# A convolution network on one core: who evicts which step of the tap matrices, where pending norms, gate weights and the sigmoid table stand

## The chip, the core and the metric

The kernel runs on one core of a Trainium2 chip. The metric is the time of one execution on the device in microseconds; the median of the runs counts. A profiled execution gives a trace besides.

## The reference, cut to what matters

An image batch of 4 images, 256 channels, 56 x 56 in fp32 goes through four layers. Each normalizes in groups of channels and adds its result to its input.

```python
x = x + involution(_gn(x), reduce_w, reduce_b, span_w, span_b)     # layer 0: 7x7, 16 groups
x = x + conv3x3_block(_gn(x), w1, bn1, w2, bn2)                    # layer 1: two 3x3 convolutions
x = x + involution_bn(_gn(x), w1, bn1, w2, b2, bn2)                # layer 2: 7x7, 16 groups, norms, relu
x = x + gates(_gn(x), W, b)                                        # layer 3
```

An involution computes, for each group of 16 channels and each pixel, its own 7 x 7 kernel (two 1 x 1 convolutions of the input, `kern = span_w @ h + span_b`), and sums `kern * patches` over the 49 taps. Layer 3 has a gate by channel, `sigmoid(cf @ W.T + b)`, where `cf` is the real mean of a Fourier transform over the image and so the image's first pixel, and a gate by pixel, the real Fourier transform of the mean over channels; the output is `x * cf + x * sf`.

## The kernel before, in words

**Units and stages.** `involution_layer` runs twice, with layer 0 and with layer 2; between them `conv_layer` does layer 1. An involution works through 8 units: 4 images b, and of each two blocks cb of 128 channels. Below, unit 0 to 7 of a layer is unit `2 * b + cb`. A unit has two stages.

*Tap phase* (`tap_matrices`, L560). 32 steps n = 0..31. In each, TensorE makes six matmuls (L571) from `z_sb` and `hp` into a PSUM tile of two banks (`two_banks`); then the tile is evicted into `kt` with the bias `zb_sb` added. Every third step, those with `n % 3 == 0` (L579), ScalarE evicts in six activations (L582); in the others VectorE does in one addition (L589). After step n, the hooks of n are called: small pieces of other work, put there by hand with `place(hooks, g, at)`. A generator g makes its next piece at each place of the list.

*Apply stage* (`apply`, L601). For each of 7 column strips tx, 112 matmuls (L613) of `xw` and `kt` go into two PSUM tiles; ScalarE (L626 or L628) and VectorE (L633, L640) or GpSimd (L638) bring the result into the image block. After each strip `next_windows` transposes a later strip (L398), ScalarE copies it to `xw` (L399), and DMAs of SP and GpSimd fill the shifted windows (L405, L407); `next_strip` normalizes the next strip, on GpSimd in layer 0 (L381) and on ScalarE in layer 2 (L379). Column statistics (`column_sums`, L1067) go to VectorE.

**PSUM.** One pool `banks` has 4 slots of two banks. The steps, the small matmuls of the hooks (`one_bank` takes a whole slot) and the apply stage share it.

**Order.** `in_order` fixes the order of each engine as the program is written, so that an instruction that waits holds up all behind it on its engine.

**The hooks that matter.** `norm_steps` (L200 to L223) makes the group norm of a block in six pieces: aggregate on VectorE (L204), matmul (L207), four VectorE operations (L210 to L215), matmul (L218), the inverse root on VectorE and GpSimd (L138, L139), shift (L222). Its places for the block just finished are steps 2, 6, 7, 11, 12, 13 (L989). In layer 0, units 1, 3 and 5 also make the norm of the next image's first block. In units 1 and 2 of layer 2 the norms of the last image of layer 1 that are still pending have the places 19, 20, 22, 23, 25, 26 (L990 to L992).

In layer 2 `channel_mean` (L668) makes, at steps 13 and 17, the mean over channels of the block that has just been finished: matmuls (L696), two ScalarE activations (L704), and two stores by SP (L707) with a load back (L708) into `m2_of`. `gate_factors` (L711) makes an image's gates when both of its blocks are finished, that is in units 2, 4 and 6: at step 17 it loads the 256 x 256 weights `w3` in two DMAs of 128 KB on SP (L716), at 24 it multiplies them with the first pixels (L723) and ScalarE applies the sigmoid (L730), at 27, 28, 30 and 31 it makes the gate by pixel (L739 to L763). The weights lie in a dead part of the image block (`dead`, L660), which must first be stored (L1082) and summed over channels (L696). The next image's load (L275) takes that block later. `gate_chunk` (L768) applies the gates to stored blocks on GpSimd in pieces of 8 rows during the units that follow; its gate map `sfb` (L773, L774) has two buffers.

The last image's gate factors have their first place at step 20 of unit 7 and their second after the last apply stage.

At its start, layer 0 has a ScalarE copy (L310) ahead of all else on that engine.

Of the kernel before, what the change touches and what calls it, by code (L numbers as in the profile page):

```python
# [10 lines left out]
F32 = mybir.dt.float32  # L11
AF = mybir.ActivationFunctionType
# [4 lines left out]
P = 128  # L17
B, C, H, W = 4, 256, 56, 56
NB = C // P
# [52 lines left out]
def net_kernel(  # L72
# [207 lines left out]
    def involution_layer(layer, xin, xout, red, span, sb, xs_of, ahead=None, pending=None):  # L280

        with ExitStack() as es:
# [23 lines left out]
            if layer == 0:  # L306
                load(0, 0, (2, 2, 2, 1))
                load(0, 1, (2, 2, 2, 1))

                nc.scalar.copy(norm_sb[:, 3, B - 1, 1, :], mhalf)  # L310

            red_sb = wpool.tile([P, NB, 2, R], F32, name="red_sb")

# [246 lines left out]
            def tap_matrices(b, cb, hooks):  # L560

                hp = h_of[b]
                kt = big.tile([Q, GB, TP // PB, NT, PB], F32, name="kt")
                for n in range(GB // 2 * TP // PB):
                    gp, pb = divmod(n, TP // PB)
                    ps = two_banks()
                    for k in range(PB):
                        py, px = divmod(pb * PB + k, TX)
                        z0 = ZF - py * QX - px
                        for i in range(2):  # L570
                            nc.tensor.matmul(  # L571
                                ps[:Q, i, k * NT : (k + 1) * NT],
                                z_sb[i * R : (i + 1) * R, cb * GB // 2 + gp, z0 : z0 + Q],
                                hp[i * R : (i + 1) * R, py, px].rearrange("p a t -> p (a t)"),
                                start=True,
                                stop=True,
                            )
                    g0, p0 = 2 * gp, pb * PB
                    if n % 3 == 0:  # L579
                        for i in range(2):  # L580
                            for k in range(PB):
                                nc.scalar.activation(  # L582
                                    kt[:, g0 + i, pb, :, k],
                                    ps[:Q, i, k * NT : (k + 1) * NT],
                                    AF.Identity,
                                    bias=zb_sb[:, cb * GB + g0 + i, p0 + k : p0 + k + 1],
                                )
                    else:
                        nc.vector.tensor_tensor(  # L589
                            kt[:, g0 : g0 + 2, pb],  # L590
                            ps[:Q, :, : PB * NT].rearrange("q i (k t) -> q i t k", k=PB),
                            zb_sb[:, cb * GB + g0 : cb * GB + g0 + 2, p0 : p0 + PB]
                            .unsqueeze(2)
                            .to_broadcast([Q, 2, NT, PB]),
                            ALU.add,
                        )
                    for h in hooks.get(n, ()):
                        h()
                return kt
# [68 lines left out]
            def channel_mean(b, cb):  # L668
# [39 lines left out]
                nc.sync.dma_start(m2_of[cb], m_dram[b][cb].rearrange("j (r w) -> (j r) w", w=W))  # L708
                yield

            def gate_factors(b):  # L711


                w3_sb = [dead(b, 1, 4 * CR * W + ci * C, C) for ci in range(NB)]
                for ci in range(NB):
                    nc.sync.dma_start(w3_sb[ci], w3[ci * P : (ci + 1) * P])  # L716
                cf = small.tile([P, NB], F32, name="cf")
                cf_of[b] = cf
                yield
                for co in range(NB):  # L720
                    ps = one_bank()
                    for ci in range(NB):
                        nc.tensor.matmul(  # L723
                            ps[:, 0:1],
                            w3_sb[ci][:, co * P : (co + 1) * P],
                            first_of[b][:, ci : ci + 1],
                            start=(ci == 0),
                            stop=(ci == NB - 1),
                        )
                    nc.scalar.activation(  # L730
                        cf[:, co : co + 1], ps[:, 0:1], AF.Sigmoid, bias=cp[:, co, L3_B : L3_B + 1]
                    )
                yield

                ps = one_bank()
                for i in range(2):
                    at = slice(i * R, i * R + W)
                    for cb in range(NB):
                        nc.tensor.matmul(  # L739
                            ps[at, :H],  # L740
                            m2_of[cb],
                            sin_sb if i else cs2_sb[:H],
                            start=(cb == 0),
                            stop=(cb == NB - 1),
                        )
                yield
                for i in range(2):
                    at = slice(i * R, i * R + W)
                    nc.vector.tensor_copy(half[at], ps[at, :H])
                yield  # L750

                ps = one_bank()
                nc.tensor.matmul(ps[:H, :W], half, cs2_sb, start=True, stop=True)
                scale = small.tile([P, NB], F32, name="gscale")
                bias = small.tile([P, NB], F32, name="gbias")
                nc.vector.tensor_mul(scale, cf, norms[3][b][0])
                nc.vector.tensor_scalar_add(scale, scale, 1.0)
                nc.vector.tensor_mul(bias, cf, norms[3][b][1])
                gate_of[b] = scale, bias
                yield  # L760
                sf = small.tile([H, W], F32, name="sf", bufs=1)
                nc.vector.tensor_copy(sf, ps[:H, :W])
                nc.sync.dma_start(sf_dram[b].rearrange("j (r w) -> (j r) w", w=W), sf)  # L763
                yield
# [3 lines left out]
            def gate_chunk(b, j, cb):  # L768

                rstd, shift = norms[3][b]  # L770
                at = slice(j * CR * W, (j + 1) * CR * W)
                if cb == 0:
                    sf_of[b] = work.tile([P, CR * W], F32, name="sfb", bufs=2)  # L773
                    nc.gpsimd.dma_start(sf_of[b], sf_dram[b][j : j + 1].to_broadcast([P, CR * W]))  # L774
                sf = sf_of[b]
                xs = gx_tile()
                nc.gpsimd.dma_start(xs, xout[b][cb][:, at])
                yield
                xn = work.tile([P, CR * W], F32, name="gn", bufs=1)
                nc.gpsimd.tensor_scalar(  # L780
                    xn, xs, rstd[:, cb : cb + 1], shift[:, cb : cb + 1], ALU.mult, ALU.add
                )

                scale, bias = (t[:, cb : cb + 1] for t in gate_of[b])
                nc.gpsimd.tensor_scalar(xs, xs, scale, bias, ALU.mult, ALU.add)
                nc.gpsimd.tensor_tensor(xn, xn, sf, ALU.mult)
                nc.gpsimd.tensor_tensor(xs, xs, xn, ALU.add)
                nc.gpsimd.dma_start(ov[b, cb][:, at], xs)
                yield
# [140 lines left out]
            def place(hooks, g, at):  # L930

                for n in at:
                    hooks.setdefault(n, []).append(step(g))
# [50 lines left out]
            for u, (b, cb) in enumerate(units):  # L984
                hooks = hooks0 if u == 0 else {}
                if prev is not None:
                    pb, pc, st, last_sums = prev
                    hooks.setdefault(1, []).append(last_column(last_sums))
                    place(hooks, norm_of(layer + 1, pb, pc, st), (2, 6, 7, 11, 12, 13))  # L989
                    if layer == 2 and u < 3:  # L990
                        g = norm_of(2, B - 1, u - 1, pending[1][u - 1])
                        place(hooks, g, (19, 20, 22, 23, 25, 26))  # L992
                    if layer == 2:
                        place(hooks, channel_mean(pb, pc), (13, 17))
                        if pc == 1:
                            place(hooks, gate_factors(pb), (17, 24, 27, 28, 30, 31))
                        elif pb == B - 1:
                            factors = gate_factors(pb)
                            place(hooks, factors, (20,))
                            hooks.setdefault(21, []).append(lambda pb=pb: last_dft(pb))  # L1000
                            hooks.setdefault(22, []).append(last_ones)
                            place(hooks, first_half(pb), (28, 29))
                    if layer == 2 and cb == 1 and b > 0:
                        for n in (16, 22, 28):
                            hooks.setdefault(n, []).extend((next_gate, next_load))
# [705 lines left out]
```

## Time and profile before

| | us |
|---|---|
| median of 3 runs | 1826.7 (1824.32 to 1828.33) |
| profiled execution, device time | 1834.67 |
| its span | 1832.9 |
| layer 0, first tap matmul | 39.19 |
| layer 2, first tap matmul | 1266.1 |
| tap phase of units 1, 2 of layer 0 | 25.12, 23.69 |
| tap phases of units 1 to 7 of layer 2 | 30.71, 35.20, 27.53, 30.64, 27.65, 33.39, 28.42 |

A tap phase is counted from the start of its first matmul record (L571) to the start of its last one. The mean granted clock of TensorE is 0.976 of full speed.

A line of a timeline has the start (us from the span's start), how long the group took, engine, line of the kernel, operation, output and inputs with their sizes, how many instructions, and in brackets the idle time of the engine before it and what ended it. PE is TensorE's matmul, PEld its load of weights, DVE VectorE, ACT ScalarE, POOL GpSimd, SP SyncE. A line of the costliest groups has the busy time and the mean duration in ns, then the idle time of the engine just before the group. A line of a table by stretches has the stretch, its length, each engine's busy time with its number of instructions (PE, PEld, DVE, ACT, POOL), the granted clock, the share of the DMA engines and GB/s. Durations come from the one profiled execution.

### The profile page before, as it was taken

What the parts mean: (1) busy time and instruction counts of PE and PEld (TensorE: products, weight loads), DVE (VectorE), ACT (ScalarE), POOL (GpSimd) and SP (SyncE); (2) the same over time, 40 slices, a digit from 0 to 9 for tenths busy, and PEclk for the clock granted to TensorE, in tenths of its full rate; (3) what the DMA queues carried; (4) which work ended last, traced back from release to release, by engine and by line L of the source; (5) the groups of instructions that cost most, each with busy time, mean ns of one, the idle gap of its engine ahead of it and who ended that gap; (6) DMA issues with size and microseconds to landing.
All of it is one profiled execution on the core that took longest, in us unless ns stands there. A gap on an engine that the chain in (4) does not pass through costs nothing.

```text
span 1832.9 us, 55841 instructions
## 1 busy us (share of the span) xinstructions
PE 1726.3 (94%) x24034; PEld 1518.9 (83%) x24034; DVE 1379.0 (75%) x2729; ACT 845.9 (46%) x1981; POOL 429.6 (23%) x626
## 2 busy tenths in 40 slices
PE   7999999999889999999999999997999899999888
PEld 6898889888878988998899889885877777887776
DVE  3787777776589988898888988874777677677674
ACT  3566556565533222223123212114667567576554
POOL 2333432245210000000000000000000563672681
PEclk9999999999989999999999999998999999999996
DMA  2545534454651101111111210222533665764743
GB/s 84 156 154 161 175 111 149 142 159 141 185 175 47 58 35 58 68 58 51 50 60 61 73 36 33 79 90 66 159 124 128 202 200 168 216 217 131 201 140 105
DMA packets 66003, 215.75 MB, mean 118 GB/s; under 512 B 13237, under 2 KB 20926, under 8 KB 62046
## 3 DMA queue, kind: packets, MB, share of 16 engines
q1 hardware_dynamic: 48718, 145.24, 25.3%
q0 software_dynamic: 14688, 64.78, 11.0%
q8 instruction: 189, 3.10, 0.7%
q10 hardware_dynamic: 2352, 2.18, 0.4%
q14 instruction: 56, 0.46, 0.1%
HBM read 76.30 MB, written 49.15 MB: 68 GB/s over the span
## 4 chain that ended last, share of the span: by engine, by line
PE 77%; DVE 9%; ACT 6%; DMA 4%; issue 2%; SPq 1%; POOL 0%; ACTq 0%; DVEq 0%; POOLq 0%
PE mm L1482 19%; PE ps L571 17%; PE ps L613 16%; PE mm L1400 10%; PE mm L1371 5%; PE ps L398 4%; ACT kt L582 3%; DMA xw<-xw 3%; PE ps L450 2%; DVE kt L589 2%; DVE un L633 1%; ACT xw L399 1%; ACT hp L469 1%; DVE res L1475 1%; PE ps L696 1%
## 5 line engine op out<-in xcount | busy, mean ns | idle before, releaser
L613 PE MATMUL ps<-kt,xw 126*32 126x48 f32 (+1 forms) x12544 | 382.5, 236 | 46.3 <-issue 18.8
L613 PEld LDWEIGHTS ps<-kt,xw 126*32 126x32 f32 (+1 forms) x12544 | 343.5, 122 | 91.7 <-issue 51.5
L571 PE MATMUL ps<-hp,z_sb 64*126 64x133 f32 x6144 | 392.3, 281 | 14.8 <-ACT kt L582 6.8
L571 PEld LDWEIGHTS ps<-hp,z_sb 64*126 64x126 f32 x6144 | 369.7, 187 | 33.2 <-ACT kt L582 12.2
L1482 PE MATMUL mm<-v,u_sb 128*128 128x280 f32 (+1 forms) x1728 | 385.0, 384 | 3.5 <-DVE v L1307 3.5
L589 DVE TENSOR_TENSOR kt<-ps,zb_sb 126x798 f32<-126x798 f32 x336 | 319.8, 982 | 90.4 <-PE ps L571 89.9
L1482 PEld LDWEIGHTS mm<-v,u_sb 128*128 128x128 f32 x1728 | 327.5, 190 | 57.9 <-DVE v L1307 3.8
L582 ACT ACTIVATE kt<-ps,zb_sb 126x133 f32<-126x133 f32 x1056 | 307.5, 442 | 94.6 <-PE ps L571 94.0
L1400 PE MATMUL mm<-v,u_sb 128*128 128x252 f32 (+1 forms) x936 | 212.4, 388 | 3.5 <-DVE v L1291 3.5
L1400 PEld LDWEIGHTS mm<-v,u_sb 128*128 128x128 f32 x936 | 178.0, 191 | 34.2 <-issue 3.5
L633 DVE SCALAR_TENSOR_TENSOR un<-ps,s,un 128x240 f32<-128x240 f32 x224 | 102.5, 458 | 97.0 <-ACT un L628 92.8
L1519 POOL DMA_DIRECT2D x<-xs x24 | 13.1, 547 | 683.2 <-DVE xs L1518 427.4
L633 DVE SCALAR_TENSOR_TENSOR un<-ps,par_sb,un 128x240 f32<-128x240 f32 x224 | 98.2, 457 | 90.9 <-ACT un L626 86.7
L1467 ACT ACTIVATE res<-xs,shift,norm_sb 128x1120 f32<-128x1120 f32 (+1 forms) x24 | 30.2, 1259 | 235.6 <-DVE xs L1518 107.3
L399 ACT COPY xw<-ps 126x896 f32<-126x896 f32 x112 | 101.7, 908 | 48.6 <-PE ps L398 40.8
L638 POOL TENSOR_TENSOR xs<-un,xs 128x240 f32<-128x240 f32 x112 | 72.3, 666 | 199.4 <-DVE un L633 199.4
L398 PE MATMUL ps<-ident_sb,strip_sb 128*126 128x128 f32 x784 | 112.1, 284 | 0.2 <-DVE un L633 0.2
L626 ACT ACTIVATE un<-ps,par_sb 128x240 f32<-128x240 f32 x112 | 50.3, 449 | 120.6 <-PE ps L613 115.5
L628 ACT ACTIVATE un<-ps,bn_t,s 128x240 f32<-128x240 f32 x112 | 60.2, 539 | 93.1 <-PE ps L613 89.9
L139 POOL TENSOR_TENSOR norm_sb<-norm_sb,mhalf 128x1 f32<-128x1 f32 x32 | 19.8, 620 | 344.1 <-DVE norm_sb L138 344.1
L1371 PE MATMUL mm<-xs,u_sb 128*128 128x126 f32 (+1 forms) x792 | 98.5, 277 | 1.3 <-DVE xs L1334 0.9
L1371 PEld LDWEIGHTS mm<-xs,u_sb 128*128 128x128 f32 x792 | 94.4, 191 | 2.4 <-issue 1.0
(254 smaller groups left out, 2000.6 us busy)
## 6 DMA issues: line engine op xcount, KB each, us to landing
xw<-xw SPq DMA_DIRECT2D x168, 252.0 KB
xw<-xw SPq DMA_DIRECT2D x224, 126.0 KB
xw<-xw POOLq DMA_DIRECT2D x56, 252.0 KB, 4.6
xs<-x SPq DMA_DIRECT2D x24, 560.0 KB
x<-xs POOLq DMA_DIRECT2D x8, 1568.0 KB, 8.0
xs<-x SPq DMA_DIRECT2D x8, 1568.0 KB
xs<-in_x_dram SPq DMA_DIRECT2D x6, 1568.0 KB
x<-xs SPq DMA_DIRECT2D x6, 1568.0 KB
```

The costliest lines, as they stand in the source:

```text
L398: nc.tensor.transpose(ps[:Q, k * P : (k + 1) * P], flat[:, k * Q : (k + 1) * Q], ident_sb)
L399: nc.scalar.copy(xw[:, :NSB, :], ps[:Q, : NSB * P].rearrange("q (n c) -> q n c", n=NSB))
L571: nc.tensor.matmul(ps[:Q, i, k * NT : (k + 1) * NT], z_sb[i * R : (i + 1) * R, cb * GB // 2 + gp, z0 : z0 + Q], hp[i * R : (i + 1) * R, py ...
L582: nc.scalar.activation(kt[:, g0 + i, pb, :, k], ps[:Q, i, k * NT : (k + 1) * NT], AF.Identity, bias=zb_sb[:, cb * GB + g0 + i, p0 + k : p0 ...
L589: nc.vector.tensor_tensor(kt[:, g0 : g0 + 2, pb], ps[:Q, :, : PB * NT].rearrange("q i (k t) -> q i t k", k=PB), zb_sb[:, cb * GB + g0 : cb ...
L613: nc.tensor.matmul(v[m * j : m * j + m, i, :, k * TP : (k + 1) * TP], xw[:, window(ty), m * j : m * j + m], kt[:, ng * j : ng * j + ng, :, ...
L628: nc.scalar.activation(part, o[0], AF.Identity, bias=bn["t4"][:, cb : cb + 1], scale=bn["s4"][ng][:, 0, cb : cb + 1])
L633: nc.vector.scalar_tensor_tensor(part, o[e], s, part, ALU.mult, ALU.add)
L638: nc.gpsimd.tensor_tensor(dst, u, dst, ALU.add)
L1371: nc.tensor.matmul(ps[:, co * m : (co + 1) * m], u[ci][:, co * P : (co + 1) * P], v2[:, e, : n // 2, ci * WT : (ci + 1) * WT], start=(ci = ...
L1400: nc.tensor.matmul(ps, u1_sb[:, ci, dy, k, co * P : (co + 1) * P], v[:, k, dy * NB + ci : (dy + n - 1) * NB + ci + 1 : NB, :], start=(j == 0),
L1482: nc.tensor.matmul(ps, u2_sb[:, ci, dy, k, co * P : (co + 1) * P], v[:, k, dy * NB + ci : (dy + n - 1) * NB + ci + 1 : NB, :], start=(j == 0),
```

## The change

Four edits. ScalarE evicts the steps with `n % 3 == 2` in place of `n % 3 == 0`: steps 2, 5, ... 29, ten in a phase, in both layers. The pending norms of layer 1 take places 15, 19, 20, 24, 25, 26. For all but the last image `gate_factors` loads its weights into the two buffers of the gate map, at step 8 in place of step 17. The first ScalarE operation of layer 0 is a sigmoid of the same operand in place of a copy (what it writes is overwritten later); the built program then has one table load on ScalarE, at that place, where the one before has a second at L730.

```diff
-                nc.scalar.copy(norm_sb[:, 3, B - 1, 1, :], mhalf)
+                nc.scalar.activation(norm_sb[:, 3, B - 1, 1, :], mhalf, AF.Sigmoid)
...
-                    if n % 3 == 0:
+                    if n % 3 == 2:
                         for i in range(2):
                             for k in range(PB):
                                 nc.scalar.activation(
...
+            def new_sf():
+                return work.tile([P, CR * W], F32, name="sfb", bufs=2)
+
             def gate_factors(b):
 
 
-                w3_sb = [dead(b, 1, 4 * CR * W + ci * C, C) for ci in range(NB)]
+                w3_sb = [new_sf()[:, :C] if b < B - 1 else dead(b, 1, 4 * CR * W + ci * C, C) for ci in range(NB)]
                 for ci in range(NB):
                     nc.sync.dma_start(w3_sb[ci], w3[ci * P : (ci + 1) * P])
...
-                    sf_of[b] = work.tile([P, CR * W], F32, name="sfb", bufs=2)
+                    sf_of[b] = new_sf()
...
                     if layer == 2 and u < 3:
                         g = norm_of(2, B - 1, u - 1, pending[1][u - 1])
-                        place(hooks, g, (19, 20, 22, 23, 25, 26))
+                        place(hooks, g, (15, 19, 20, 24, 25, 26))
                     if layer == 2:
                         place(hooks, channel_mean(pb, pc), (13, 17))
                         if pc == 1:
-                            place(hooks, gate_factors(pb), (17, 24, 27, 28, 30, 31))
+                            place(hooks, gate_factors(pb), (8, 24, 27, 28, 30, 31))
```

On SP the two weight loads then stand right behind the store of the finished block and ahead of the channel mean's stores, its load and the next image's load. PSUM slots are given out anew along the changed order.

## Prediction

> **What bounds the kernel now.** I read the page first (shares, costliest groups), then the chain of work that ended last for the second involution layer (from 1240 us on), then timelines of single tap phases.
>
> ```profile
> PE 1726.3 (94%) x24034; PEld 1518.9 (83%) x24034; DVE 1379.0 (75%) x2729; ACT 845.9 (46%) x1981; POOL 429.6 (23%) x626
> ...
> L571 PE MATMUL ps<-hp,z_sb 64*126 64x133 f32 x6144 | 392.3, 281 | 14.8 <-ACT kt L582 6.8
> ```
>
> TensorE is the bound, and in a tap phase (32 steps, L571) it waits only where an eviction (L582, L589) has not freed a PSUM slot. 16 units of 192 matmuls give 6144 records, two for each. The last steps of a tap phase in layer 0:
>
> ```profile
> 183.95 1.75 ACT L582 ACTIVATE kt<-ps,zb_sb 126x133 f32<-126x133 f32 x6 [0.37 <-PE ps L571]
> 184.51 0.40 PE L613 MATMUL ps<-kt,xw 126*64 126x96 f32 x2
> 184.63 0.99 DVE L589 TENSOR_TENSOR kt<-ps,zb_sb 126x798 f32<-126x798 f32 x1 [0.17 <-PE ps L571]
> 185.75 3.08 PEld L613 LDWEIGHTS ps<-kt,xw 126*64 126x64 f32 x110 [1.04 <-ACT kt L582]
> ```
>
> Step 30 is ScalarE's, step 31 VectorE's; both end near 185.7, and the apply stage then goes on. The head of a tap phase in layer 2:
>
> ```profile
> 1327.66 0.91 ACT L399 COPY xw<-ps 126x896 f32<-126x896 f32 x1 [0.39 <-PE ps L398]
> ...
> 1328.46 1.04 ACT L379 ACTIVATE strip_sb<-xs,norm_sb 128x784 f32<-128x784 f32 x1
> ...
> 1329.41 3.33 ACT L582 ACTIVATE kt<-ps,zb_sb 126x133 f32<-126x133 f32 x12
> ...
> 1331.20 1.41 PE L571 MATMUL ps<-hp,z_sb 64*126 64x133 f32 x20 [0.64 <-ACT kt L582]
> ```
>
> ScalarE makes a window copy and a strip before step 0's eviction, and TensorE stands. Later in units 1 and 2 of layer 2, and in unit 6:
>
> ```profile
> 1347.93 0.35 PE L207 MATMUL ps<-mv,gavg_sb 128*128 128x1 f32 x2 [0.94 <-DVE mv L204]
> ...
> 1351.68 0.35 PE L218 MATMUL ps<-d,gavg_sb 128*128 128x1 f32 x2 [1.15 <-DVE d L215]
> ```
> ```profile
> 1421.93 1.28 ACT L730 ACT_TABLE_LOAD   x1
> ```
> ```profile
> 1687.33 0.35 PE L723 MATMUL ps<-first,xs 128*128 128x1 f32 x2 [1.43 <-DMA xs<-in_w_dram]
> 1688.04 0.84 PE L723 MATMUL ps<-first,xs 128*128 128x1 f32 x6 [0.36 <-DMA xs<-in_w_dram]
> ```
> ```profile
> 1687.00:1690.00 3.00, 2.31 (x18) 2.24 (x20) 0.00 (x0) 1.22 (x5) 0.00 (x0) 0.79 0.15 41
> 1690.00:1693.00 3.00, 3.00 (x38) 2.82 (x34) 1.98 (x2) 0.22 (x1) 0.00 (x0) 0.64 0.00 0
> ```
>
> Matmuls in order wait for a statistic, a table load or the gate weights; the last two lines (busy time of each engine, then granted clock) show that TensorE also runs slowly after such a stop.
>
> **The Trainium skill.** "Perfetto Trace Analysis", Identifying Performance Opportunities: a gap that repeats on the busiest engine can mean too few PSUM buffers. The trace agrees: 0.64 us at the layer-2 head shown, with four slots for the steps. "TensorE: Matmul & The Clock Gate", What's actually happening: after an idle window the array gets half its clock until it has been busy. The trace agrees in kind: 0.79 and 0.64 granted after the wait at 1687, and 0.58 from 1422 to 1425. "ScalarE: Activation LUTs", What ACT_TABLE_LOAD costs: 1283 ns and a drain, together some 2.66 us. The trace shows 1.28 us; the drain it doesn't show. Same page, Table sets: cheap functions are in every set; in the trace six evictions take 1.76 us before and after the load at 1421.93.
>
> **How the parts are costed.** I walk the 32 steps forward in the order that each kernel gives its engines and PSUM slots. Rows: a TensorE step 0.70 us (0.79 after a stop), its eviction can begin 0.90 later (1.00 after a stop); ScalarE's six evictions 1.76, VectorE's one 0.98 (0.91 apart in a row); a step starts 0.05 after its slot's last reader. The walk of before gives 25.2 and 23.8 us for layer 0's odd and even units (trace 25.1 and 23.7) and 30.4, 27.3, 28.0 for units 1, 3, 7 of layer 2 (30.7, 27.5, 28.4), so differences of it can be trusted to a few tenths.
>
> **Eviction order.** Three steps take TensorE 2.09, ScalarE 1.76, VectorE 1.89: nothing changes in the middle. ScalarE has 10 groups instead of 11, VectorE 22 instead of 21. *Tail, each of 16 units:* steps 30 and 31 both fall to VectorE. Step 30 is ready 0.68 before 31, the second starts 0.91 after the first, so 0.23 later than now and ends that much later; now ScalarE ends 0.08 after VectorE, so the loss is 0.14. *Head, layer 0:* in even units waits of 0.05+0.12+0.31 (steps 7, 8, 12) become 0.26+0.22 (7, 14): even. In units 1, 3, 5 VectorE also has the next image's statistic (L349, 0.61) ahead of step 0, so it begins at 1.49 instead of 1.00; behind it stand the evictions of steps 0, 1, 3 and 4 and the norm's pieces. The walk finds 1.50 of waits against 0.92: +0.5 and the tail. Layer 0: 5x0.14 + 3x0.62 = +2.6 us. *Layer 2:* step 4 waits 0.79 for ScalarE's step 0; now VectorE frees that slot and ScalarE begins at step 2, when strip and copy are done. In unit 1, counted from its first matmul: now ScalarE has copy and strip until 1.86, ends step 0 at 3.60, and step 4, due at 2.88, begins at 3.65; after, VectorE begins step 0 at 1.23, behind its column statistic, and ends it at 2.21. Given back in part at step 7, where the norm takes a slot (0.2 to 0.6). The 0.54 wait at step 22, behind ScalarE's channel-mean copies, goes. Units 3, 5: -0.6 each; unit 7: -1.6.
>
> **Norms.** In units 1 and 2 each of the two matmuls now comes four steps (2.8 us) after its statistic's VectorE work, instead of one; 0.99+1.19 us of waiting go, and the VectorE work between evictions is spread. With the eviction order the walk gives unit 1: -3.3.
>
> **Sigmoid.** The load at 1421.93 (1.28 us, ahead of the gate's activations, on which TensorE's slots wait) disappears; the one at the start is there anyway. In unit 2 the walk of norms, order and load together gives -3.35; the load's part is 0.8.
>
> **Weights.** In units 2, 4, 6 the two loads move on SP from behind the channel-mean's stores to ahead of them, right behind the 1568 KB store of the block. They now wait for the last reader of the gate map's buffers on GpSimd; behind them on SP stand m's stores, then the next image's load. In the trace GpSimd's last such reads end by 1532.9 and 1661.3, before SP reaches that place (after 1536.5 and 1666.7): no wait, and some 10 us of cover while the store drains (DMA share 1.00 from 1537 to 1542, 0.07 after). With that cover gone today's wait returns. The walk, with order: unit 4 -0.36, unit 6 -2.0. Next late would be m2 (issued at 1552.8, used near 1557.5); 0 to 1 us, taken as 0, since TensorE shows no wait for it. GpSimd's first gate-map load then waits for the weight matmul at hook 24, long past. The image load no longer waits for that matmul and goes earlier: 0.
>
> **The clock.** Without the stops in units 2 and 6 the slow steps go: in unit 6 three steps took 0.70+0.63+0.32 us over the normal, in unit 2 0.78+0.79+0.42 less 0.54 the walk has as a wait. I take 1.5 each (bounds 0 and 2): -3.0.
>
> **Sum.** Layer 2: -(3.3+3.35+0.6+0.35+0.6+2.0+1.6) = -11.8, with the clock -14.8. Layer 0: +2.6. The first unit of layer 2 has 1.5 us of statistics at hook 3 in VectorE's queue, and unit 0 an own head: 0, bounds -0.7 and +0.7. Net -12.2. The profiled execution took 1834.67 us (span 1832.9), so 1822.5 there; the median of the runs shown is 1826.7, so **1814.5**.
>
> **Rivals.**
> *The forecast*: 1814.5, chance 0.66; own range 1810 to 1819 (clock 3 us, slots 0.2 a unit, the odd heads).
> *The gain dissolves in the apply stages* of units 2, 4, 6: the chain has 7.1% of 593 us, 42 us, in window transfers, and if these keep their own pace, the 5.7+3.0 us of those units are swallowed: -3.5, 1823. For: waits of 6 to 9 us for them. Against: the windows are copied in step with the stage itself, and traffic is near nothing (share 0.00 to 0.07) in the stretch that shrinks. 0.12.
> *Layer 0 loses nothing*, VectorE's order works out better than walked, and heads gain more: -17, 1809.5. 0.10.
> *The weights come no earlier* (SP held by the gate map's buffers): unit 6 and unit 4 keep their waits, 2.6+1.5 lost: 1818.5. Against: the GpSimd times above. 0.06.
> *VectorE becomes the bound*: it fills 1.89 of 2.09 us a trio, regains only 0.2 a trio, and now begins every phase with the old columns' work ahead of two evictions. If the backlog reaches the end, each of 16 units pays it; above 14.8/16 = 0.93 us a unit the change is slower; at 1.5 it is 1836. For: unit 1's +0.6. Against: four slots between, and the walk's even units. 0.06.
>
> This kernel's measurement can tell about 0.2% from no change (3.7 us). Faster by more: 0.90; within: 0.05; slower: 0.05. The range 1809 to 1821 leaves out the dissolved case and VectorE's.
>
> **What would show it.** Tap phases: unit 1 of layer 2 at 27 us instead of 30.7, unit 2 at 30 instead of 35.2, unit 6 near 29.5 instead of 33.4; layer 0's odd units at 25.6, even ones unchanged, apply going on 0.15 later. No table load past the start, no granted clock under 1 near those gates, no TensorE wait for w_dram before the last image. The forecast is wrong if layer 0's units grow by 1 us each, or if layer 2's units don't shorten as their taps do.

## The result and the profile after

| | before | after |
|---|---|---|
| median of 15 runs each, us | 1825.4 (1815.21 to 1835.53) | 1815.04 (1810.34 to 1822.32) |
| ratio after to before | | 0.9952, 95% interval 0.9932 to 0.9971 |
| span of the profiled execution, us | 1832.9 | 1811.2 |
| mean granted clock of TensorE | 0.976 | 0.982 |

The change makes the kernel faster by 0.48% of 1825.4, that is 8.8 us (5.3 to 12.4 by the interval; the two medians differ by 10.4). The spans differ by 21.7 us, more than the change is worth. Of this, 6.2 us lie in the stretch from unit 7's apply stage in layer 0 through layer 1 to layer 2's first tap matmul, in which the edits change nothing. That stretch took 781.6 to 788.9 us over the fourteen kernels profiled for this study. The seven apply stages of layer 2 took 236.2 to 244.8 us in all. Single spans are therefore not compared below. What is compared is the tap phase: from its first tap matmul to its last (the "taps"), and then to the moment at which the apply stage goes on (the "resume"). In layer 0 such a phase repeats within 0.05 us in nearly every unit.

Tap phase plus resume, in us, with what the forecast's walk gave:

| unit | before | after | difference | forecast |
|---|---|---|---|---|
| layer 0, unit 0 | 28.59 | 27.59 | -1.00 | +0.14 |
| layer 0, units 1, 3, 5 | 26.57, 26.59, 26.58 | 27.15, 27.16, 26.83 | +0.58, +0.57, +0.25 | +0.62 each |
| layer 0, units 2, 4, 6, 7 | 25.15 each | 25.32 each | +0.17 each | +0.14 each |
| layer 2, unit 0 | 30.77 | 31.49 | +0.72 | 0 |
| unit 1 | 32.16 | 28.83 | -3.33 | -3.3 |
| unit 2 | 36.65 | 31.31 | -5.34 | -3.35 - 1.5 |
| unit 3 | 28.98 | 29.33 | +0.35 | -0.6 |
| unit 4 | 32.09 | 30.95 | -1.14 | -0.35 |
| unit 5 | 29.11 | 30.15 | +1.04 | -0.6 |
| unit 6 | 34.84 | 31.14 | -3.70 | -2.0 - 1.5 |
| unit 7 | 29.88 | 30.24 | +0.36 | -1.6 |

The differences sum to -9.9 us. Without the -1.2 in the taps of layer 0's unit 0, which come from the clock at its start (see below), they sum to -8.7, near the 8.8 us of the timed runs. That they meet so closely is in part luck: each profile is one execution, and units 2 and 6 of the one before each hold 3.41 us at half clock that other executions may lack.

First the page of the changed kernel: engines, then the costliest groups.

```profile
PE 1716.0 (95%) x24034; PEld 1510.2 (83%) x24034; DVE 1398.0 (77%) x2745; ACT 819.5 (45%) x1884; POOL 429.0 (24%) x626
...
L571 PE MATMUL ps<-hp,z_sb 64*126 64x133 f32 x6144 | 383.7, 278 | 14.6 <-DVE kt L589 5.9
```

Sixteen evictions have moved from ScalarE to VectorE (2745 against 2729). The idle time ahead of the tap matmuls is 14.6 us (14.8 before), but VectorE's evictions now end the largest part of it (5.9 us), where ScalarE's did (6.8).

The end of unit 2's tap phase in layer 0, after:

```profile
183.08 1.48 ACT L582 ACTIVATE kt<-ps,zb_sb 126x133 f32<-126x133 f32 x5
...
183.55 1.89 DVE L589 TENSOR_TENSOR kt<-ps,zb_sb 126x798 f32<-126x798 f32 x2 [0.23 <-PE ps L571]
...
184.12 0.40 PE L613 MATMUL ps<-kt,xw 126*64 126x96 f32 x2
185.55 1.17 PEld L613 LDWEIGHTS ps<-kt,xw 126*64 126x64 f32 x19 [1.24 <-ACT kt L582]
185.58 1.26 PE L613 MATMUL ps<-kt,xw 126*64 126x96 f32 x17 [1.06 <-DVE kt L589]
```

Steps 30 and 31 are one group of two VectorE evictions, ending at 185.44. The apply stage goes on 1.66 us after the last tap matmul; before it was 1.45.

The head of unit 1 of layer 2, after:

```profile
1322.49 4.79 PE L571 MATMUL ps<-hp,z_sb 64*126 64x133 f32 x78
1322.59 0.91 ACT L399 COPY xw<-ps 126x896 f32<-126x896 f32 x1 [0.37 <-DMA xw<-xw]
...
1323.40 1.04 ACT L379 ACTIVATE strip_sb<-xs,norm_sb 128x784 f32<-128x784 f32 x1
...
1323.99 1.87 DVE L589 TENSOR_TENSOR kt<-ps,zb_sb 126x798 f32<-126x798 f32 x2
...
1324.86 1.75 ACT L582 ACTIVATE kt<-ps,zb_sb 126x133 f32<-126x133 f32 x6 [0.42 <-PE ps L571]
```

VectorE takes steps 0 and 1 while ScalarE still copies and normalizes. TensorE's first stretch has 78 records, six and a half steps; before, it stopped ahead of step 4 for a ScalarE eviction (0.64 us). The pending norm in unit 1, and the gate weights in unit 6:

```profile
1340.30 0.38 PE L207 MATMUL ps<-mv,gavg_sb 128*128 128x1 f32 x2
...
1344.30 0.38 PE L218 MATMUL ps<-d,gavg_sb 128*128 128x1 f32 x2
```
```profile
1671.99 1.05 PE L726 MATMUL ps<-first,sfb 128*128 128x1 f32 x8
```
```profile
1671.50:1674.50 3.00, 2.88 (x40) 2.67 (x40) 1.70 (x3) 1.84 (x8) 0.00 (x0) 1.00 0.00 0
1674.50:1677.50 3.00, 3.00 (x52) 2.67 (x50) 2.38 (x3) 1.76 (x6) 0.00 (x0) 1.00 0.00 0
```

None of the three groups has a bracket: no wait for a statistic (0.94 and 1.15 us before) and none for the weights (1.43 and 0.36). The granted clock stays at 1.00. In the list of groups ScalarE has one table load left, at L310:

```profile
L310 ACT ACT_TABLE_LOAD x1 | 1.3, 1283 | 2.9 <-issue 2.9
```

So the pending norms, the weights, the table and the head of unit 1 went as forecast. Units 3, 5 and 7 did not: they were to give 2.8 us and cost 1.75.

### The profile page after: what moved, and what is told of

It reads as the page before. It is cut to its first block, busy times and chain, and to the rows that moved or that the text cites. A ratio compares the mean times of both kernels' runs of the same rounds, so it can differ in the third digit from the quotient of the medians.

```text
span 1811.2 us, 55765 instructions
## 1 busy us (share of the span) xinstructions
PE 1716.0 (95%) x24034; PEld 1510.2 (83%) x24034; DVE 1398.0 (77%) x2745; ACT 819.5 (45%) x1884; POOL 429.0 (24%) x626
## 4 chain that ended last, share of the span: by engine, by line
PE 74%; DVE 17%; ACT 3%; DMA 3%; issue 2%; SPq 1%; POOL 1%; ACTq 0%; DVEq 0%; POOLq 0%
PE mm L1485 19%; PE ps L613 16%; PE ps L571 14%; PE mm L1403 10%; DVE kt L589 6%; PE mm L1374 5%; PE ps L398 4%; DVE un L633 2%; DMA xw<-xw 2%; PE ps L450 2%; DVE st L1070 1%; ACT kt L582 1%; ACT hp L469 1%; DVE res L1478 1%; PE ps L696 1%
## 5 line engine op out<-in xcount | busy, mean ns | idle before, releaser
L571 PE MATMUL ps<-hp,z_sb 64*126 64x133 f32 x6144 | 383.7, 278 | 14.6 <-DVE kt L589 5.9
L571 PEld LDWEIGHTS ps<-hp,z_sb 64*126 64x126 f32 x6144 | 363.2, 185 | 31.1 <-DVE kt L589 8.5
L589 DVE TENSOR_TENSOR kt<-ps,zb_sb 126x798 f32<-126x798 f32 x352 | 332.9, 980 | 58.5 <-PE ps L571 58.3
L582 ACT ACTIVATE kt<-ps,zb_sb 126x133 f32<-126x133 f32 x960 | 280.7, 442 | 109.2 <-PE ps L571 109.0
```

The source lines that it names most:

```text
L571: nc.tensor.matmul(ps[:Q, i, k * NT : (k + 1) * NT], z_sb[i * R : (i + 1) * R, cb * GB // 2 + gp, z0 : z0 + Q], hp[i * R : (i + 1) * R, py ...
L582: nc.scalar.activation(kt[:, g0 + i, pb, :, k], ps[:Q, i, k * NT : (k + 1) * NT], AF.Identity, bias=zb_sb[:, cb * GB + g0 + i, p0 + k : p0 ...
L589: nc.vector.tensor_tensor(kt[:, g0 : g0 + 2, pb], ps[:Q, :, : PB * NT].rearrange("q i (k t) -> q i t k", k=PB), zb_sb[:, cb * GB + g0 : cb ...
```

## Experiments

**Which edit brings the gain.** Three kernels have one edit each and one has everything but the eviction order, run on one chip beside 59 runs of the kernel before (1824.8 us). The sigmoid alone came with the next set, on another chip.

Eviction order alone:

```diff
-                    if n % 3 == 0:
+                    if n % 3 == 2:
```

> The kernel before with ScalarE on the steps n % 3 == 2 and nothing else of the change. Theory (the time follows the sum of TensorE's waits in the tap phases): layer 0 about +1 us (tails +0.2 in 16 units, odd units +0.4, unit 0 -1), units 1, 3, 5, 7 of layer 2 between -0.6 and +1, the others up to +0.7: in all +1 to +4 us, ratio 1.001. Rival (the order is where the gain comes from): -5 us or more, ratio under 0.9975.

Measured: 1825.28 us, ratio 1.0007 (0.9995 to 1.0018). Phases in layer 0 +2.4 us, in layer 2 -2.0. The order alone brings nothing that shows.

Norm places alone:

```diff
-                        place(hooks, g, (19, 20, 22, 23, 25, 26))
+                        place(hooks, g, (15, 19, 20, 24, 25, 26))
```

> The kernel before with the pending norms at places 15, 19, 20, 24, 25, 26 and nothing else. Theory: the tap phases of units 1 and 2 of layer 2 shorten by 1.7 us each by the walk, all others stay to 0.1 us; -3.3 us, ratio 0.998. Rival (the order is needed for it): under 1 us in each.

Measured: 1819.99 us, ratio 0.9971 (0.9956 to 0.9985). The taps of unit 1 took 28.38 us (before 30.71), those of unit 2 33.37 (35.20): -4.2 in all. Unit 6, which the edit doesn't touch, took 30.92 where the profile of before has 33.39. The wait for the weights there is 1.24 us against 1.79, and the profile of before has 3.41 us at half clock behind it, this run none.

Weights alone:

```diff
+            def new_sf():
+                return work.tile([P, CR * W], F32, name="sfb", bufs=2)
...
-                w3_sb = [dead(b, 1, 4 * CR * W + ci * C, C) for ci in range(NB)]
+                w3_sb = [new_sf()[:, :C] if b < B - 1 else dead(b, 1, 4 * CR * W + ci * C, C) for ci in range(NB)]
...
-                            place(hooks, gate_factors(pb), (17, 24, 27, 28, 30, 31))
+                            place(hooks, gate_factors(pb), (8, 24, 27, 28, 30, 31))
```

> The kernel before with the gate weights loaded into the gate map's buffers at place 8 and nothing else. Theory: unit 4 of layer 2 -0.6, unit 6 -2.0 and -1.5 more for the slow clock after the wait; unit 2, where the weights had landed in time, 0; no TensorE wait for w_dram before the last image; -4 us, ratio 0.998. Rival (weights come no earlier, SP held by the gate map's buffers): 0.

Measured: 1819.99 us, ratio 0.998 (0.9968 to 0.9992). Unit 6's taps took 29.69 us. With this edit unit 6's taps take 29.4 to 30.5 us in each of the ten kernels that have it, and 30.9 to 34.8 in the four that don't: what is removed is a wait of 1.2 to 1.8 us, and the half clock that two of these four have in unit 6 (3.41 and 6.83 us).

Everything but the order:

```diff
-                    if n % 3 == 2:
+                    if n % 3 == 0:
```

> The changed kernel with ScalarE back on n % 3 == 0. Theory: layer 0 as before to 0.1 us a unit; units 1, 2, 4, 6 of layer 2 by the walk -1.7, -2.3, -0.6, -2.0 and 1.5 each for the slow clock in 2 and 6: -9.6 us, ratio 0.9947, as much as the whole change gave (0.9952). Rival (the norms need the order): units 1 and 2 keep half their waits, -6 us, ratio 0.9967.

Measured: 1814.69 us, ratio 0.9944 (0.9925 to 0.9963). That is the whole change's time, without the new order. By phases the order costs 2.9 us in layer 0 (of it 0.6 in unit 0) and gains 1.2 in layer 2, where the forecast's walk counts on more. With the sigmoid alone, below, the four single edits lie together 0.0034 under a ratio of 1 (by their intervals, some 0.003 either way), and the whole change 0.0048: that the edits help each other is not shown.

Sigmoid alone:

```diff
-                nc.scalar.copy(norm_sb[:, 3, B - 1, 1, :], mhalf)
+                nc.scalar.activation(norm_sb[:, 3, B - 1, 1, :], mhalf, AF.Sigmoid)
```

> The kernel before with one edit: the first ScalarE operation of layer 0 is the sigmoid. Theory: the table load of 1.28 us in unit 2 of layer 2 goes, and that tap phase ends 0.8 us earlier than 35.2 us, with up to 1.5 us more if the slow clock after it goes too; all other phases stay. About 1 to 2 us of 1825, so a ratio of 0.999 to 0.9995. Unit 0 of layer 0 tells where its 27.1 us (before, order alone, norms alone, weights alone) against 25.5 to 25.9 us (changed kernel, all but the order) come from: if the sigmoid at the head makes the difference, it is near 25.5 here; if it is the clock at the start, by chance, either can come. Rival: the load wasn't on the path, and unit 2 stays at 35.2 us.

Measured: 1824.46 us, ratio 1.0008 (0.9989 to 1.0026). The second load is gone and unit 2's taps took 33.18 us, 2.0 less. Of this, 0.33 us is TensorE's wait behind the load; the rest fits the half clock that the profile of before has there for 3.41 us and this run has not. Over whole executions a gain of that size can't be told from none.

Unit 0 of layer 0 took 25.50 here, which by itself would have pointed to the sigmoid. Four later kernels have the sigmoid too and took 27.1. The table by stretches has the cause, first before, then after:

```profile
39.00:42.00 3.00, 2.81 (x32) 2.84 (x34) 0.49 (x1) 2.00 (x8) 0.00 (x0) 0.68 0.01 3
42.00:45.00 3.00, 3.00 (x32) 2.59 (x31) 2.04 (x10) 0.93 (x2) 0.00 (x0) 0.75 0.01 3
```
```profile
39.00:42.00 3.00, 2.67 (x40) 2.57 (x41) 1.61 (x2) 0.63 (x3) 0.00 (x0) 1.00 0.00 0
42.00:45.00 3.00, 3.00 (x49) 2.83 (x48) 2.34 (x11) 2.38 (x8) 0.46 (x1) 1.00 0.02 5
```

The column after the five engines is the granted clock: 0.68 and 0.75 in one, 1.00 in the other. Such values are means. In the fourteen traces the clock is either 1.00 or 0.50, and all its changes in a trace lie on a grid of 3.413 us. In before, one period of that grid is slow here:

```profile
36.68:40.09 3.41, 1.25 (x18) 1.10 (x18) 0.00 (x0) 2.56 (x10) 0.00 (x0) 1.00 0.00 0
40.09:43.50 3.41, 3.41 (x30) 3.17 (x27) 1.99 (x6) 1.76 (x6) 0.00 (x0) 0.50 0.02 5
```

Six of the fourteen kernels start at full clock (25.5 to 25.9 us for this phase; 27.1 in the others), with and without the new order. All six have the sigmoid, and none of the four kernels without it is among them, so the lengths alone leave it in question. The grid sorts them without it. In the eight slow ones the phase begins 0.50 to 1.43 us before the end of a period, and TensorE was busy for 0.37 to 0.42 of that period; in the six others it begins 1.49 to 1.76 us before, and the share is 0.43 to 0.51. The ten kernels with the sigmoid lie anywhere between 0.50 and 1.76 us, and the four without it between 0.83 and 1.43, so I count the -1.2 of unit 0 as no part of the change.

**Why units 3, 5 and 7 give nothing.** GpSimd in unit 3, after, and then VectorE in the same stretch:

```profile
1464.58 0.56 POOL L139 TENSOR_TENSOR norm_sb<-norm_sb,mhalf 128x1 f32<-128x1 f32 x1 [10.25 <-DVE norm_sb L138]
1465.14 0.71 POOL L783 TENSOR_SCALAR gn<-gx,norm_sb 128x448 f32<-128x448 f32 x1
1465.94 0.72 POOL L788 TENSOR_SCALAR gx<-gx,gscale,gbias 128x448 f32<-128x448 f32 x1
1466.62 1.13 POOL L789 TENSOR_TENSOR gn<-gn,sfb 128x448 f32<-128x448 f32 x1
```
```profile
1465.30 0.55 DVE L222 SCALAR_TENSOR_TENSOR norm_sb<-gm,norm_sb 128x1 f32<-128x1 f32 x1
1465.89 0.28 DVE L674 TENSOR_SCALAR first<-xs,norm_sb 128x1 f32<-128x1 f32 x1
1466.08 1.71 DVE L685 TENSOR_SCALAR mean<-cmean,norm_sb 128x32 f32<-128x32 f32 x2
1467.71 1.87 DVE L589 TENSOR_TENSOR kt<-ps,zb_sb 126x798 f32<-126x798 f32 x2
```

The gate pieces are written into the program at step 16, but GpSimd waits for nothing there and begins them right behind its inverse root. VectorE's shift (L222) ends at 1465.85, exactly with GpSimd's L783. The two scalings for the channel mean (L685), 0.23 us each elsewhere, take 0.62 and 1.19, and each ends 0.04 us after GpSimd's operation (L788 at 1466.66, L789 at 1467.75). Behind them stand the evictions of steps 15 and 16 (L589, the last line, begun at 1467.71). TensorE's channel mean (L696) needs step 15's slot, and begins at 16.31 us of the phase.

The old order is held too, but less. The same two scalings in unit 3 of before, and the whole line there (minimum, median and maximum in ns):

```profile
1478.15 1.35 DVE L685 TENSOR_SCALAR mean<-cmean,norm_sb 128x32 f32<-128x32 f32 x2
```
```profile
L685 DVE TENSOR_SCALAR mean<-cmean,norm_sb x14: 228/234/1203, 1341.1 to 1749.5; 128x32 f32<-128x32 f32 x14
```

Of the two only one is held there, 1.20 us in unit 3 and 0.91 in units 5 and 7; the other keeps 0.23 or 0.24. Behind them stands step 14's eviction. L696 begins at 15.98, 16.10 and 16.18 us of units 3, 5 and 7 in before, and at 16.31, 17.13 and 16.53 after. In units 3 and 7 the new order is 0.6 and 0.5 us ahead when step 13 begins, and behind at this point; unit 5 is 0.2 us behind at step 13 already.

The Trainium skill, "SBUF — State Buffer", section "Who interferes with whom", says that VectorE and GpSimd share a pair of ports which the first to start holds for its whole instruction while the other fully blocks; among what can contend it counts VectorE's tensor_scalar, in the modes that use both ports, and operations with two inputs in SBUF against a GpSimd operation that reads SBUF. The trace agrees: 0.23 becomes 1.19 us, with the ends 0.04 us apart, and the evictions, which take one input from PSUM, keep their 0.98. In which mode the scalings run it doesn't show.

A direct test leaves GpSimd's four arithmetic operations out of three of each image's fourteen gate pieces, those that fall at this place; these pieces of the output are stored without their gate.

```diff
+                if NB * j + cb not in (5, 6, 7):
                     xn = work.tile([P, CR * W], F32, name="gn", bufs=1)
                     nc.gpsimd.tensor_scalar(
...
```

> The changed kernel without the four GpSimd operations of three of each image's fourteen gate pieces (the sixth, seventh and eighth; those pieces are stored as they were loaded). These are the pieces that GpSimd begins right after its inverse root in the tap phases of units 3, 5 and 7 of layer 2. Theory: a running GpSimd operation holds VectorE's small ones; without them the shift (L222) takes 0.15 us in place of 0.55 and the two means (L685) 0.23 each in place of 0.62 and 1.19, step 15 is evicted near 13.7 instead of 15.3 us (unit 3), TensorE's wait of 0.9 us in each for the mean goes, and the three tap phases shorten from 27.7, 28.5 and 28.6 to about 26.5, 27.2 and 27.4 us. Rival: the long means have another cause (the queue, the operand's place); then they keep 0.6 and 1.2 us and the three phases stay within 0.3 us.

Measured: one execution, 1807.25 us (kernel before 1825.07). The answers for the line L685, of the changed kernel and of this one:

```profile
L685 DVE TENSOR_SCALAR mean<-cmean,norm_sb x14: 229/236/1193, 1335.7 to 1728.7; 128x32 f32<-128x32 f32 x14
...
  PE ps L693: 2.7, 3
```
```profile
L685 DVE TENSOR_SCALAR mean<-cmean,norm_sb x14: 229/231/235, 1336.7 to 1725.8; 128x32 f32<-128x32 f32 x14
```

No scaling is held any more, and TensorE's wait for them (2.7 us in three places, the second line) is gone. The taps of units 3, 5 and 7 took 26.44, 27.24 and 26.36 us (27.67, 28.49, 28.58): -1.2, -1.25 and -2.2, and L696 begins at 15.11, 15.91 and 14.35. In unit 7, 0.9 of this arises before the scalings, which start at 12.96 us of the phase instead of 13.88. So the hold at the scalings costs the new order 1.2 to 1.3 us in each of the three units; that cause is shown.

**Taking the scalings off VectorE.** With the whole change:

```diff
-                    nc.vector.tensor_scalar_mul(c, cmean, t[:, cb : cb + 1])
+                    nc.scalar.mul(c, cmean, t[:, cb : cb + 1])
```

> The changed kernel, with the two scalings of the mean's column in channel_mean (L685) made by ScalarE in place of VectorE. Theory: in units 3, 5 and 7 of layer 2 a running GpSimd operation holds these two on VectorE (0.62 and 1.19 us in place of 0.23 each), steps 15 and 16 are both evicted behind them, and TensorE waits for the mean (L693) and for a slot (L696); so on ScalarE, which the GpSimd operation doesn't hold, they take about 0.3 us, step 15 is evicted near 13.7 instead of 15.3 us, and each of the three tap phases shortens by 0.9 to 1.3 us, from 27.7, 28.5 and 28.6 to about 26.6, 27.3 and 27.4: 3 us in all, 1812 where the changed kernel has 1815. The other phases stay within 0.2. Rival: it is not the GpSimd operation but the load on VectorE's queue as such; then ScalarE's means are as late or its next step pays (step 17 or 20), and the three phases stay within 0.3 us.

Measured: 1815.04 us, ratio 0.9947 (0.9924 to 0.997): nothing gained. On ScalarE no scaling is held (0.32 us each), but units 3, 5 and 7 got only 0.36, 0.86 and 0.65 shorter, and units 2, 4 and 6 longer by 0.5, 1.2 and 0.8, of which 0.5 each arises at steps 14 to 18 and the rest at the head. ScalarE in unit 4:

```profile
1534.75 0.63 ACT L685 ACTIVATE mean<-cmean,norm_sb 128x32 f32<-128x32 f32 x2 [1.18 <-POOL norm_sb L139]
1535.29 3.31 ACT L582 ACTIVATE kt<-ps,zb_sb 126x133 f32<-126x133 f32 x12
```

At step 13 the scalings stand ahead of step 14's eviction in ScalarE's order and wait there for the norm; the eviction begins 0.99 us after its last matmul's start, 0.32 in the changed kernel. I had looked only at the engine that gets rid of the work, not at what stands behind it on the engine that takes it.

The same with everything but the order:

> Every edit but the eviction order, with the means on ScalarE as well. There the two means stand ahead of the evictions of steps 14 and 16 on VectorE, and TensorE's matmuls for the channel mean wait for step 14's slot (eviction ends at 16.1 us in unit 3). Theory: units 3, 5 and 7 shorten by 0.5 to 1 us each from 27.8, 27.5 and 28.6, so some 2 us, 1812.5 where all but the order has 1814.7. Rival: with ScalarE's own step 15 next in its queue the means delay that one instead, and the gain is under 0.5 us in all.

Measured: 1812.42 us, ratio 0.9932 (0.9902 to 0.9962). Units 3, 5 and 7: -0.43, -0.40 and -0.61, where the theory gave 0.5 to 1 each. The old order thus loses less to the hold than the new one. Unit 2 took 32.50 us instead of 30.87, mostly for a reason that the windows show (this kernel, then everything but the order, each from TensorE's stop at the gate):

```profile
1409.50:1412.50 3.00, 2.38 (x26) 2.29 (x27) 0.90 (x1) 1.01 (x5) 0.00 (x0) 0.73 0.76 315
1412.50:1415.50 3.00, 3.00 (x40) 2.70 (x40) 1.20 (x4) 1.24 (x5) 0.55 (x1) 0.71 0.00 0
```
```profile
1413.00:1416.00 3.00, 2.38 (x39) 2.21 (x40) 1.34 (x3) 0.85 (x5) 0.21 (x1) 1.00 0.71 298
1416.00:1419.00 3.00, 3.00 (x48) 2.62 (x48) 2.37 (x6) 1.92 (x7) 0.34 (x1) 1.00 0.00 0
```

Both stop for 0.62 us in those 3 us (TensorE busy 2.38). The first then runs at half clock from 1410.85 to 1414.27, one period of the grid; the other stays at 1.00. In the first the stop (1409.70 to 1410.32) lies within one period, in the other a period ends in the middle of it, at 1413.41. What exactly decides is not shown: in unit 2 of other kernels a period with TensorE busy for 0.66 of it is followed by half clock in one trace and by full clock in four.

With the new order in layer 2 alone, and the scalings on ScalarE:

```diff
-                    if n % 3 == 2:
+                    if n % 3 == (0 if layer == 0 else 2):
```

> The changed kernel with the new eviction order in layer 2 only (layer 0 keeps ScalarE on the steps n % 3 == 0), and the means on ScalarE. Theory: layer 0's units go back to 25.1 and 23.7 us with the apply stage going on 1.46 us later (0.2 less in each unit, 0.4 less in the odd ones), 2.6 to 2.9 us in all, and layer 2's are as in the run with the means on ScalarE alone: together some 5.5 us under the changed kernel, 1809.5, a ratio to before of 0.991 to 0.992. Rival: layer 0's loss is swallowed by the apply stages behind it, and this is no faster than the run with the means on ScalarE alone.

Measured: 1812.68 us, ratio 0.9931 (0.991 to 0.9953). Layer 0's units are back at 25.1 and 23.7 us with a resume of 1.45, 4.0 us under the run with the order in both (1.55 of it in unit 0's taps, most of which is the clock at its start). Layer 0's seven apply stages took 230.5 us against 229.1 in that run, and 228.4 to 230.7 over the fourteen kernels, so whether they swallow a part is not settled. The whole is 3 us short of the forecast: layer 2's phases sum to 244.2 us, as in the run with the scalings on ScalarE (244.9), where 3 us less were forecast.

**Versions from what was found.** The scalings go to ScalarE in units 3, 5 and 7 only, one step later, behind step 14's eviction; the order is new in layer 2 alone.

```diff
-                    nc.vector.tensor_scalar_mul(c, cmean, t[:, cb : cb + 1])
+                    (nc.scalar.mul if b > 0 and cb == 0 else nc.vector.tensor_scalar_mul)(c, cmean, t[:, cb : cb + 1])
...
-                        place(hooks, channel_mean(pb, pc), (13, 17))
+                        place(hooks, channel_mean(pb, pc), (14 if pb > 0 and pc == 0 else 13, 17))
```

> The changed kernel with the new order in layer 2 only, and with the means of units 3, 5 and 7 alone on ScalarE and one step later (14), behind step 14's eviction on that engine; the even units and unit 1 keep VectorE. Theory: in the last set of runs ScalarE's means stood ahead of step 14's eviction and waited there for VectorE's shift, which cost 0.5 to 0.8 us in the even units and part of the gain in the odd ones. So units 3, 5 and 7 come to about 26.5, 26.8 and 27.1 us (27.3, 27.6 and 27.9 with the means on ScalarE at step 13), and units 2, 4 and 6 return to 29.9, 29.5 and 29.7; 5 to 6 us under the changed kernel with layer 0's 2.6, near 1809.5, ratio 0.9915. Rival: the means now come so late that the channel mean waits for them as it did for VectorE: odd units within 0.3 us of the changed kernel's.

Measured: 1810.37 us, ratio 0.992 (0.99 to 0.994). Units 3, 5 and 7: 26.58, 27.16 and 27.14, within 0.4 us of the forecast (unit 3 with 1.88 us at half clock at its head); units 2 and 6 29.90 and 29.65, as forecast; unit 4 30.79 instead of 29.5, for a reason not looked into (28.8 to 31.4 over the fourteen kernels).

The same without the new order:

> The same treatment of the means, with the old eviction order in both layers: it differs from the run beside it by layer 2's order alone. Forecast of the order's worth once the hold is gone: 0.6 in units 3 and 5 and 1.6 in unit 7, some 1.2 in unit 1, together 4 to 5 us in layer 2 with the heads of units 2, 4 and 6; this run then is at 1813 to 1814 where the other is at 1809.5. Rival, from the runs so far (order against no order, 1 to 2 us in layer 2): what the head gains is used up by later waits whatever the means do, and the two runs are within 2 us.

Measured: 1809.96 us, ratio 0.992 (0.9907 to 0.9934). The whole times are alike, as the rival had it. In the phases of layer 2 the order is worth 3.0 us (taps 4.1, resumes -1.0). Of the taps' 4.1, 2.5 lie in unit 2, where this kernel again has the half clock (0.58 in the mean from 1412 to 1415); the changed kernel stops there for only 0.34 us, and the six kernels with all four edits in layer 2 took 29.9 to 30.4 us. In units 3, 5 and 7, resumes included, the order is worth 1.3 us here, where neither order has its scalings on VectorE. My 4 to 5 us were too many by the phases, and whether 3 us are there in the whole time is not settled: intervals of 0.27% and 0.4% don't tell them.

Last, ScalarE takes step 30 in place of 29 in layer 2:

```diff
-                    if n % 3 == 2:
+                    if (n % 3 == 0) if layer == 0 else (n == 30 or n % 3 == 2 and n < 29):
```

> As the run with the order in layer 2 and late means, but ScalarE takes step 30 in place of step 29 in layer 2, so that the last two steps are shared by both engines again. Theory: two VectorE evictions at the end let the apply stage go on 1.66 us after the last tap matmul where it was 1.45; here it goes back to 1.45 in units 0, 1, 3, 5 and 7 and stays near 1.45 in the others: 0.2 us in five units, 1 us in all, near 1808.5, ratio 0.991. Rival: three VectorE evictions in a row (27 to 29) delay a late step by as much, and nothing is gained.

Measured: 1810.54 us, ratio 0.9912 (0.9897 to 0.9928). The resume is 1.45 to 1.46 again in units 0, 3, 5 and 7 (1.66 without), 1.59 in unit 1, and the taps of units 1, 3 and 7 are 0.5 to 0.7 us shorter too. Most of that is no work of the edit: step 7 already begins 0.6, 0.4 and 0.5 us earlier, where both kernels evict alike. That a whole execution is quicker than in the two runs above can't be told. Against before its interval lies below that of the change as it was made (0.9932 to 0.9971).

## Why the prediction was right, and where not

The forecast was 1814.5 us and the measurement 1815.04, but the gain of 12.2 us that stood behind it was too large: the timed runs give 8.8, the medians 10.4. The median met in part by luck, because the kernel before, in more runs, stands at 1825.4 and not at 1826.7. The term that failed is "Eviction order". By the steps:

- **Norms**: with the order, unit 1 -3.33 against -3.3. Right; alone it brings -2.3 and -1.8, so most of the edit's worth doesn't need the order.
- **Sigmoid, Weights, The clock**: units 2 and 6 together -9.0 against -8.35. Right in mechanism; that the size fits is in part luck. The loads come early enough, and TensorE waits for no weights before the last image. But the profile of before has the longest of four such waits (1.79 us with both stops; the others 1.24 to 1.65), and one period at half clock in each of the two units. Unit 2 has none in two of the other six kernels with the old order in layer 2, unit 6 none in two of the other three that load the weights late. The table load's part is 0.33 us of wait and not 0.8.
- **Eviction order, layer 0**: +2.3 without unit 0's start, against +2.6. The tail costs 0.21 us and not 0.14, the heads of units 1 and 3 +0.37 and not +0.48, unit 5's +0.03 (+0.25 in two other kernels with this order). In unit 0 the order costs a further 0.4 when both kernels start at full clock (25.92 against 25.50), nothing when both start slowly.
- **Eviction order, layer 2**: this step failed, in its sentence "Units 3, 5: -0.6 each; unit 7: -1.6". Measured +0.35, +1.04 and +0.36, an error of 4.5 us. The costs on record have no row for a VectorE operation that is held; in the walk I gave the two scalings 0.23 us each, their median, in each unit. The line's maximum, 1.2 us, stood in the trace of before, and in just these units: GpSimd holds them. In the new order both are held (0.62 and 1.19 us), TensorE's channel mean begins later than before, and the head's gain is gone; taking the hold away brings 1.2 to 1.3 us in each unit. That the walk of before matched the trace within 0.4 us hid this: there one scaling of two is held, and taking both off VectorE brought the old order only 0.4 to 0.6 us a unit. The hold is not all of the error. With the scalings of both orders moved to ScalarE the new order is worth 1.3 us in these units and not 2.8, so the walk also made too much of the head; in unit 5 the gain is lost before step 13. How the 4.5 us divide is not settled.
- **Unit 0 of layer 2**: +0.72, at its bound. Its taps take 27.9 to 30.1 us over the fourteen kernels, and two things sort them: how long the phase runs at half clock, and the order. The old order takes 27.89 us with 2.92 us at half clock and 29.32 with 6.20; the new one 28.95 with 3.41 and 30.10 with 5.79. At 5.2 us it is 28.99 against 29.83, so the order costs some 0.8 us here that the sum had at 0.
- **Rivals**: the apply stages of units 2, 4 and 6 didn't lengthen (103.7 us before, 102.2 after; 100.6 to 109.2 over the fourteen kernels). The weights came earlier. Layer 0 did lose. VectorE did not become the bound: it adds 0.21 us a unit, where 0.93 would have decided.

The parts thus sum to -9.9 us in the phases, -1.2 of it from the clock at the start, where -12.2 was forecast.

## What to carry to other kernels

Price an operation by its durations at the place in question, not by the median of its line: a minimum and maximum of 0.23 and 1.2 us on one line were here the sign that something held it, and the groups of the other engines that end at the same time told what. Moving evictions between two engines gains only as far as the next point where TensorE needs a result of one of them; where that point is set by something else, the head's gain is lost there and the tail's cost stays. A wait for a transfer and the half clock around a stop differ between traces of kernels that are alike at that place: look at several before one of them is put into a sum, and compare phases only where the clock ran alike.

## What the runs showed of the hardware

- A running GpSimd operation on SBUF holds VectorE's small ones on SBUF to its end (0.23 to 1.19 us, 0.15 to 0.55), while ScalarE's on the same operands keep 0.32 us and VectorE's evictions from PSUM 0.98.
- TensorE's granted clock is 1.00 or 0.50 in all fourteen traces, and its changes in a trace lie on a grid of 3.413 us. At the first tap phase the clock halved for one period where TensorE had been busy for 0.37 to 0.42 of the period before (eight kernels), and didn't at 0.43 to 0.51 (six); the slow start costs 1.2 to 1.6 us.
- Around the same stop of 0.62 us TensorE kept its full clock in one execution and ran at half clock for 3.41 us in another, whose phase was 1.6 us longer.
